# Softmax row sums moved ahead of the next group's first attention product

## The chip, the cores and the metric

One core of one Trainium2 chip. The metric is the device time of one execution in microseconds.

## The reference

Eight images of 512 channels and 32 x 32 pixels pass through a group norm, a 1 x 1 convolution, two bottleneck blocks, and a last 1 x 1 convolution with a residual. Each block is a 3 x 3 convolution, an attention over 1024 pixels with four heads of 64 channels, and a 1 x 1 convolution. What the change touches is the attention, cut to its core:

```python
qkv = conv2d(x, qkv_w, 0).reshape(b, 3, HEADS, HD, hw)
q, k, v = (qkv[:, 0], qkv[:, 1], qkv[:, 2])
logits = jnp.einsum('bhdi,bhdj->bhij', q, k + r) * HD ** (-0.5)
a = jax.nn.softmax(logits, axis=-1)
out = jnp.einsum('bhij,bhdj->bhdi', a, v)
```

## The kernel before

An attention is done in four groups (two pairs of heads, two halves of the query pixels). A group has eight key tiles, taken in pairs, so four steps. Each step computes the logits of one pair on TensorE (`l_ps`, L479), their exponentials on ScalarE (`pt`, L483), the running sum of the exponentials on VectorE (`acc`, L489 and L491), and, one step behind, the product with v on TensorE (`av_ps`, L505), which accumulates over the group's four steps.

```python
ps_big = ...tile_pool(name="ps_big", bufs=3, space=PSUM)   # logits, sums, group norm ...
ps_av  = ...tile_pool(name="ps_av", bufs=1, space=PSUM)    # the product with v

def times_v(pair):
    ...
    if j0 == 0:
        avs[g] = ps_av.tile([P, 2, HALF], F32, tag="av", name="av_ps")
    ... # 8 matmuls (16 passes) into avs[g]                        L505
    if j0 + PAIR == NJ:                  # last step of the group: the drain
        av = avs.pop(g)
        dst = ao[:, c, ts(half, HALF)]
        nc.scalar.copy(dst, av[:, 0])                              # L512
        nc.vector.tensor_tensor(dst, av[:, 1], dst, ALU.add)       # L513

def sums(g):                             # ones @ acc, to memory for the rescale
    ps = ps_big.tile([P, NQ4], F32, tag="big", name="s_ps")
    acc = accs.pop(g)
    for at_q in range(4):
        nc.tensor.matmul(ps[at_q*32:(at_q+1)*32, :], ones[:, 0:32], ...)   # L523
    nc.scalar.copy(row, ps)                                        # L529
    nc.sync.dma_start(s_dram, row[0:P:32, :])
    return s_dram

def scale(g, rs):
    nc.vector.tensor_tensor(dst, dst, rs, ALU.mult)                # L579

for i in range(len(pairs) + 1):
    if i < len(pairs):
        added = logits(pairs[i])
        g, at_q = divmod(i, NQ)
        with tc.issue_after(added.ins):
            ...
            if at_q == 0 and g > 1:
                scale(g - 2, rss.pop(g - 2))
    if i > 0:
        times_v(pairs[i - 1])
        g, j0 = pairs[i - 1][0]
        if j0 == 0:
            if g > 0:
                s_drams[g - 1] = sums(g - 1)
            with tc.issue_after(added.ins):
                behind.get(g, lambda: None)()    # other work, group norm among it
```

(`...` stands for lines left out.) PSUM is the memory into which TensorE writes. A group's product leaves its only PSUM buffer in two halves, one copied by ScalarE (L512) and one added by VectorE (L513): this is called the drain. The rescale (L579) multiplies an older group's output by the reciprocals of its row sums. A boundary is the place where one group ends and the next begins; TensorE is "held" at a boundary when the next product has to wait for the drain. The group-norm products (`gm_ps`, `gv_ps`) are small matmuls for a later group norm.

## Time and profile before

| | before |
|---|---|
| median time | 2486.34 us (2485.52 to 2486.74, 3 runs) |
| span in the profile | 2485.1 us |
| TensorE, VectorE, ScalarE busy | 97%, 60%, 38% |
| boundaries between groups, each with one set of sums (L523) | 48 |

The page's list of costly groups gives for each: busy time, mean duration of one instruction in ns, then the idle time of the engine just before it, and what ended that idle time.

```profile
L479 PE MATMUL l_ps<-q,kr 64*64 64x512 f32 x4096 | 488.0, 594 | 8.5 <-ACT pt L483 8.5
L505 PE MATMUL av_ps<-pt,vT 64*64 64x512 f32 x4096 | 486.4, 592 | 9.0 <-DVE ao L513 7.5
```

The two products of attention cost the same. Before the second one TensorE stands idle for 9.0 us in all, 7.5 of them for VectorE's half of the drain.

In the view of line L523, the sums, ScalarE waits 71.5 us in all at 47 boundaries to copy them out. ScalarE has time to spare, so this costs nothing by itself; it shows that the sums stand late in TensorE's stream.

### The profile page before, as it was taken

To read this page: it belongs to the slowest core of one execution; us is meant where nothing else is said; L and a number is where in the kernel's file an instruction comes from. 1 tells how busy PE (TensorE), PEld (TensorE's weight loads), DVE (VectorE), ACT (ScalarE), POOL (GpSimd) and SP (SyncE) were. 2 spreads that over 40 slices of the span, in tenths; PEclk is the share of its full clock that TensorE was granted. 3 is DMA by queue.
4 is the path that set the end of the run, shared out by engine and by line. 5 is a ranking of instruction groups with operands and counts; after the bars stand their busy time and mean duration, and the time that the engine had idled before them with its cause. 6 is when DMAs were issued, how large, how long until landed. Compare 5 with 4: busy or idle time off the path is not lost.

```text
span 2485.1 us, 35553 instructions
## 1 busy us (share of the span) xinstructions
PE 2416.4 (97%) x14626; PEld 1198.2 (48%) x14626; DVE 1488.6 (60%) x2482; ACT 939.7 (38%) x1280; POOL 104.9 (4%) x355
## 2 busy tenths in 40 slices
PE   6799999999999999999999999999999999999998
PEld 4436446363463634636355363644536354363533
DVE  7678554766456664666546665566564665636654
ACT  2353522525134251443414334153431525325252
POOL 1000000000100001000010000100001000010001
PEclk9899999999999999999999999999999999999999
DMA  7124014040140402304032030502205021050102
GB/s 235 61 90 157 27 39 170 14 153 10 60 149 15 152 15 85 119 14 153 14 133 76 29 134 15 181 28 77 91 10 203 10 87 43 22 191 14 69 10 65
DMA packets 82203, 200.01 MB, mean 80 GB/s; under 512 B 27889, under 2 KB 37809, under 8 KB 69745
## 3 DMA queue, kind: packets, MB, share of 16 engines
q1 hardware_dynamic: 68080, 152.00, 17.8%
q0 software_dynamic: 11808, 45.62, 5.2%
q8 instruction: 117, 1.92, 0.3%
q14 instruction: 54, 0.43, 0.1%
q10 hardware_dynamic: 2144, 0.03, 0.0%
HBM read 167.74 MB, written 29.88 MB: 80 GB/s over the span
## 4 chain that ended last, share of the span: by engine, by line
PE 86%; DVE 5%; ACT 3%; issue 2%; DMA 0%; POOL 0%; SPq 0%; ACTq 0%; DVEq 0%
PE ps L266 33%; PE av_ps L505 15%; PE l_ps L479 14%; PE c_ps L695 13%; PE v_ps L445 4%; PE m_ps L716 4%; ACT pt L483 3%; PE s_ps L523 1%; DVE ao L513 1%; PE s_ps L541 1%; ACT t L252 1%; DVE acc L491 0%; DVE acc L489 0%; DVE v_in L325 0%; DVE st L368 0%
## 5 line engine op out<-in xcount | busy, mean ns | idle before, releaser
L483 ACT ACTIVATE pt<-l_ps 128x1024 f32<-128x1024 f32 x512 | 495.1, 1023 | 230.7 <-PE l_ps L479 230.7
L491 DVE TENSOR_TENSOR acc<-acc,pt 128x1024 f32<-128x1024 f32 x384 | 469.6, 1223 | 131.8 <-ACT pt L483 108.1
L479 PE MATMUL l_ps<-q,kr 64*64 64x512 f32 x4096 | 488.0, 594 | 8.5 <-ACT pt L483 8.5
L505 PE MATMUL av_ps<-pt,vT 64*64 64x512 f32 x4096 | 486.4, 592 | 9.0 <-DVE ao L513 7.5
L695 PEld LDWEIGHTS c_ps<-v_in,u 128*128 128x128 f32 x2688 | 302.6, 192 | 11.5 <-issue 6.7
L695 PE MATMUL c_ps<-v_in,u 128*128 128x128 f32 x2688 | 303.2, 275 | 4.2 <-DVE v_in L325 4.2
L505 PEld LDWEIGHTS av_ps<-pt,vT 64*64 64x64 f32 x4096 | 153.3, 133 | 306.1 <-issue 222.1
L479 PEld LDWEIGHTS l_ps<-q,kr 64*64 64x64 f32 x4096 | 150.2, 133 | 283.1 <-issue 259.1
L266 PE MATMUL ps<-x,w 128*128 128x512 f32 x512 | 227.8, 601 | 2.2 <-DVE x L401 2.2
L266 PE MATMUL ps<-z,qkv_sb 128*128 128x512 f32 x512 | 229.3, 595 | 0.4
L266 PE MATMUL ps<-ypad,w 128*128 128x512 f32 x512 | 227.8, 594 | 0.6 <-ACT t L252 0.6
L489 DVE TENSOR_TENSOR acc<-pt 128x1024 f32<-128x1024 f32 x64 | 78.4, 1225 | 136.8 <-ACT pt L483 136.8
L266 PEld LDWEIGHTS ps<-x,w 128*128 128x128 f32 x512 | 97.1, 192 | 130.8 <-issue 127.3
L266 PEld LDWEIGHTS ps<-ypad,w 128*128 128x128 f32 x512 | 96.5, 190 | 126.0 <-issue 124.6
L433 DVE TENSOR_TENSOR kr<-ps,rw_sb 128x512 f32<-128x512 f32 x64 | 41.2, 686 | 186.0 <-PE ps L266 186.0
L252 ACT ACTIVATE t<-ps,bh,sh 128x512 f32<-128x512 f32 x58 | 42.7, 775 | 274.6 <-PE ps L266 166.8
L266 PEld LDWEIGHTS ps<-z,qkv_sb 128*128 128x128 f32 x512 | 94.7, 190 | 107.2 <-issue 91.8
L778 DVE TENSOR_TENSOR t<-t,x_res 128x512 f32<-128x512 f32 x64 | 43.8, 690 | 170.2 <-ACT t L252 142.8
L266 PE MATMUL ps<-y,w 128*128 128x512 f32 x256 | 118.0, 599 | 4.1 <-ACT t L252 4.1
L332 ACT COPY m<-c_ps 128x256 f32<-128x256 f32 x96 | 35.5, 369 | 221.2 <-PE c_ps L695 214.7
L266 PE MATMUL ps<-ylast,w 128*128 128x512 f32 x256 | 117.2, 595 | 0.0
L445 PE MATMUL v_ps<-qkv_sb,z 128*128 128x256 f32 x512 | 115.7, 379 | 0.0
(121 smaller groups left out, 1980.9 us busy)
## 6 DMA issues: line engine op xcount, KB each, us to landing
u<-u SPq DMA_DIRECT2D x84, 1024.0 KB
w<-in_cv_w_dram SPq DMA_DIRECT2D x25, 1024.0 KB
x<-in_x_dram SPq DMA_DIRECT2D x32, 512.0 KB
x_res<-in_x_dram POOLq DMA_DIRECT2D x64, 256.0 KB, 3.8
out_dram<-t POOLq DMA_DIRECT2D x62, 256.0 KB, 2.9
u<-u_new POOLq DMA_DIRECT2D x12, 1024.0 KB, 5.4
rs<-r_dram SPq DMA_DIRECT2D x96, 128.0 KB
raw<-in_m_cv_w_dram SPq DMA_DIRECT2D x8, 576.0 KB
```

The lines of the kernel that those rows point to most:

```text
L252: return nc.scalar.activation(dst, src, AF.Silu, scale=sh[:, k : k + 1], bias=bh[:, k : k + 1])
L266: nc.tensor.matmul(ps[:, half, :], w_of(k), rhs_of(k, half), start=(k == begin), stop=(k == end))
L433: nc.vector.tensor_tensor(dst, img(ps[:, half, :]), rw, ALU.add)
L445: nc.tensor.matmul(ps[:, at, :], z[:, k, ts(j0 + at, P)], qkv_sb[:, n, k, 2 * C : 3 * C], start=(k == 0), stop=(k == NM - 1),)
L479: nc.tensor.matmul(ps[kh * HD : (kh + 1) * HD, hd, :], kr[r, c, o : o + HD], q[r, c, ts(half, HALF)], start=True, stop=True,)
L483: exp = nc.scalar.activation(pt[:, i], ps, AF.Exp, scale=SCALE)
L489: return nc.vector.tensor_tensor(accs[g], pt[:, 0], pt[:, 1], ALU.add)
L491: ins = nc.vector.tensor_tensor(accs[g], accs[g], pt[:, i], ALU.add)
L505: nc.tensor.matmul(avs[g][hd * HD : (hd + 1) * HD, kh, :], vT[r, j, o : o + HD], pt[r, i, hd, :], start=(j == 0), stop=(j == NJ - 1),)
L695: nc.tensor.matmul(ps[:, row, col, :], us[i][:, k, row, col, :], vs[i][:, k, row, col, :], start=(k == 0), stop=(k == NM - 1),)
L716: nc.tensor.matmul(pss[oc][:, half, :], m2_sb[:, n, k, ts(oc, P)], ao[:, k, ts(half, HALF)], start=(k == 0), stop=(k == NM - 1),)
L778: nc.vector.tensor_tensor(t, t, res.pop(0), ALU.add)
```

## The change

The intent: at a group boundary TensorE waits for the previous group's product to be drained before the next group's first product may overwrite its only PSUM buffer. The sums are independent work that stands right behind that product. They are put ahead of it, so that they run during the wait.

```diff
                 if i > 0:
+                    g, j0 = pairs[i - 1][0]
+                    if j0 == 0 and g > 0:
+                        s_drams[g - 1] = sums(g - 1)
                     times_v(pairs[i - 1])
-                    g, j0 = pairs[i - 1][0]
                     if j0 == 0:
-                        if g > 0:
-                            s_drams[g - 1] = sums(g - 1)
                         with tc.issue_after(added.ins):
                             behind.get(g, lambda: None)()
```

## The prediction

> **What bounds the kernel now.** I read the page first for the busy shares, then the chain of work that ended last, then the waits of the lines that the change moves, and last the timeline at a boundary between two groups, because only start times show whether TensorE loses anything there.
>
> ```profile
> PE 2416.4 (97%) x14626; PEld 1198.2 (48%) x14626; DVE 1488.6 (60%) x2482; ACT 939.7 (38%) x1280; POOL 104.9 (4%) x355
> ...
> PEclk9899999999999999999999999999999999999999
> ...
> PE 86%; DVE 5%; ACT 3%; issue 2%; DMA 0%; POOL 0%; SPq 0%; ACTq 0%; DVEq 0%
> PE ps L266 33%; PE av_ps L505 15%; PE l_ps L479 14%; PE c_ps L695 13%; PE v_ps L445 4%; PE m_ps L716 4%; ACT pt L483 3%; PE s_ps L523 1%; DVE ao L513 1%; PE s_ps L541 1%; ACT t L252 1%; DVE acc L491 0%; DVE acc L489 0%; DVE v_in L325 0%; DVE st L368 0%
> ```
>
> TensorE is busy 97% of the span at full granted clock, and 86% of the chain lies on it. So a change is worth what it takes out of TensorE's own stream of starts. The one foreign entry near the sums (L523) is L513, the VectorE half of draining the attention product (av_ps), with 1% of the chain.
>
> ```profile
> L513 DVE TENSOR_TENSOR ao<-av_ps,ao x64: 680/683/693, 130.4 to 2435.1; 128x512 f32<-128x512 f32 x64
> ...
>   PEld av_ps L505: 45.2, 48
>   PE av_ps L505: 7.5, 31
> ```
>
> These are the waits on L513: weight loads of the next product waited 45.2 us at 48 boundaries, matmuls 7.5 us at 31. The two disagree, and neither is the gain. The weight-load figure counts idle time that always lies between loads (0.28 us in the steady stream); the matmul figure leaves out the time by which the modelled matmul end (1.90 us for 16) overhangs the step to the next start (1.72 us). The timeline settles it. This is one boundary, all engines but weight loads; columns are start and duration in us:
>
> ```profile
> 458.52 1.90 PE L479 MATMUL l_ps<-q,kr 64*64 64x512 f32 x16
> 458.77 0.59 ACT L512 COPY ao<-av_ps 128x512 f32<-128x512 f32 x1 [0.64 <-PE av_ps L505]
> 459.31 0.68 DVE L579 TENSOR_TENSOR ao<-ao,rs 128x512 f32<-128x512 f32 x1
> 459.62 1.94 ACT L483 ACTIVATE pt<-l_ps 128x1024 f32<-128x1024 f32 x2 [0.27 <-PE l_ps L479]
> 459.91 0.69 DVE L513 TENSOR_TENSOR ao<-av_ps,ao 128x512 f32<-128x512 f32 x1
> 460.65 1.95 PE L505 MATMUL av_ps<-pt,vT 64*64 64x512 f32 x16 [0.23 <-DVE ao L513]
> 460.68 2.55 DVE L491 TENSOR_TENSOR acc<-acc,pt 128x1024 f32<-128x1024 f32 x2
> 462.52 0.64 PE L523 MATMUL s_ps<-acc,ones 128*32 128x256 f32 x8
> 463.09 0.39 PE L374 MATMUL gm_ps<-mv,gmat 128*128 128x4 f32 x2
> ```
>
> The logits start at 458.52 and the next group's first product at 460.65: 2.13 us, against 1.72 us for an undisturbed step. TensorE is held 0.41 us. The product has one PSUM buffer (two 512-column halves), and it comes free only when VectorE ends L513 at 460.60. VectorE is late because the rescale L579 of an older group is ahead of L513 in its queue. Then the sums run, with their inputs long ready. The work that could have filled the hole stands right behind it.
>
> **What the Trainium skill says.** "Perfetto Trace Analysis", section "Tensor Engine Instruction (MATMUL, LD_WEIGHTS)", says that the reported end of a matmul is estimated, not observed, so I count start to start. The 1.90 us blocks above that begin every 1.72 us agree. "TensorE: Matmul & The Clock Gate", "Step-by-step: what each phase is for", says matmuls stay in program order and only weight loads are pulled ahead; so the sums behind a blocked product cannot slip past it. The trace agrees: none of the 48 sums starts before its product. "TensorEngine Tiling (Array Packing)", "Key Properties", says that changing the tiling mode drains TensorE. The trace shows a price: in the case without a wait, a 64*64 block followed by the 128*32 sums takes 1.83 us to the next start, not 1.72 (+0.11), and the logits after the sums take 1.77 (+0.05). "Perfetto Trace Analysis", "Optimization Strategy", ties a repeating bubble on the saturated engine to too few buffers; the single buffer of av_ps is that here.
>
> **The change, part by part.** Nothing is added or removed. At 48 boundaries (8 images, 2 blocks, 3 boundaries) the four sums (8 passes) move from behind the next group's first 16-pass product to ahead of it. The built instruction order confirms it: on TensorE the swap alone, on VectorE nothing, on ScalarE one swap of a sums copy with a weight transform in the first image, on the DMA queue only names of scratch buffers.
>
> Will the sums themselves wait? They need the last accumulate of the old group, which precedes in VectorE's queue the first accumulate of the new one (L489, which began at 458.16, before the logits), and a buffer of the three-deep PSUM ring that an exponential freed at 458.14. In the new place they have two written-out waits, one for each; both are over by 458.2, two microseconds before the sums' turn.
>
> Cost of one boundary, from the start of the logits to the start of the following product, read from the starts of all 48:
>
> Before, held: 2.13 (logits, wait) + 1.88 (product; 0.05 more than 1.83, as its first weights could not be loaded early) + 0.57 (sums) + 1.77 (next logits) = 6.35 us. After: 1.83 (logits, switch into the sums) + 0.57 (sums) + 1.77 (product) + 1.72 (logits) = 5.89 us. The drain ends at about 2.13 after the start of the logits and the product would start at 2.40, so the whole wait is covered with 0.27 us to spare. Gain 0.46 us.
>
> Before, not held (first boundary of each attention: no older group to rescale, so L513 ends at 1.70): 1.72 + 1.83 + 0.57 + 1.77 = 5.89 us. After: the same. Gain 0.
>
> Held, with a group-norm product behind it (gm_ps or gv_ps, 128*128, at the second and third boundary of the first block of seven images, 14 in all): before, the sums shield it and it adds 0.31 us. After, it stands between a 64*64 product and 64*64 logits and must pay its own switch, so 0.11 + 0.05 us are given back (estimate from the switches above). Gain 0.30 us.
>
> The count: 16 not held (0). Of the other 32, one in the first image starts at 1.84 and has a group-norm product: 0. One starts at 2.50 because the rescale waited 0.28 us for its transfer: about 0.57. Twelve regular ones with a group-norm product: 12 x 0.30 = 3.6. Eighteen regular ones without: 18 x 0.46 = 8.3. Sum 12.5 us, or 0.5% of 2486.34.
>
> Beside this, the sums' result leaves some 2 us earlier: ScalarE's copy L529, which now idles 71.5 us in all for the sums, can follow the exponentials at once. The row sums go through memory sooner. None of it is on the path: the reciprocal L567 waited for its transfer 0.9 us in all, and ScalarE is busy 38%.
>
> **The rivals.** (1) The hole moves and is not filled: the sums wait in the new place, for VectorE or for the ring. Against it stand the times above (ready two microseconds early) and VectorE's slack at the boundary (1.62 us idle before L489). It would make the gain near 0: 2486. (2) The chain's 1% on L513 is all gain, some 25 us: 2461. Against: L513's 0.69 us mostly run while the logits still do; only 0.41 us shows in the starts. (3) The matmul wait of 7.5 us is the whole gain: 2479. Against: it misses the overhang between modelled end and next start and counts 0.23 where the starts show 0.41. (4) Switching is not symmetric: the step from the sums into the product cannot load weights early, or group norm costs more than I took. For it: the trace has no case of sums followed by a product. At 0.2 us more per boundary it would eat 9.6 of the 12.5 us: 2483. (5) The saved time becomes a wait elsewhere: row-sum transfers or the next image's weights take fixed time while TensorE arrives earlier. For it: the last rescale (L579) already waits for transfers, 57.8 us over 17 times. Against: the m_ps products that need it show no matmul idle, since the filler products lie between. Worth 1 or 2 us.
>
> **Range and chances.** Prediction 2474 us. The range 2469 to 2481 holds the sum with a give-back of half (rival 4 or 5) on one side, and a gain in the not-held boundaries or smoother exponentials on the other. A 2% gain needs 50 us, four times the sum and twice the chain's share for L513; a 2% loss would need a full microsecond more at every boundary, more than the sums take. Chances: faster by over 2% 0.01, within 2% 0.98, slower 0.01.
>
> **What would show it.** Right: logits to sums 1.83 us at nearly all 48 boundaries, sums to product 0.57, product to logits 1.77, no matmul wait of L505 on L513 but for one or two; L513 gone from the chain or far smaller; the group-norm product about 0.11 us later behind its product; ScalarE's wait for L523 far below 71.5 us. Wrong: a wait of L523 for VectorE or ScalarE (rival 1); sums to product clearly above 0.57 without a wait on L513 (rival 4); the boundaries shorter as reckoned but the span not, with new waits in the 3x3 or final products (rival 5).

## The result, and the profile after

| | before | changed |
|---|---|---|
| median time | 2486.54 us (2485.52 to 2487.82, 4 runs) | 2474.05 us (2473.74 to 2474.80, 4 runs) |
| span in the profile | 2485.1 us | 2472.6 us |

The ratio of the times is 0.995 (95% interval 0.9933 to 0.9967). Ratios here and below are the mean time of one kernel's fast runs over that of the other's of the same rounds, so not quite the ratio of the medians quoted. The medians differ by 12.5 us.

The page after the change: busy shares, the chain by engine and by line, and the same two groups (granted clock 0.993, as before 0.994).

```profile
PE 2411.5 (98%) x14626; PEld 1201.4 (49%) x14626; DVE 1488.8 (60%) x2482; ACT 934.0 (38%) x1280; POOL 104.6 (4%) x355
...
PE 93%; DVE 3%; ACT 1%; issue 0%; ACTq 0%; DVEq 0%
PE ps L266 34%; PE av_ps L505 18%; PE l_ps L479 18%; PE c_ps L695 13%; PE v_ps L445 4%; PE m_ps L716 4%; PE s_ps L523 1%; PE s_ps L541 1%; ACT t L252 1%; DVE v_in L325 0%; DVE acc L491 0%; ACT pt L483 0%; DVE st L368 0%; DVE v_in L323 0%; DVE ypad L724 0%
...
L479 PE MATMUL l_ps<-q,kr 64*64 64x512 f32 x4096 | 486.1, 592 | 8.5 <-ACT pt L483 8.5
L505 PE MATMUL av_ps<-pt,vT 64*64 64x512 f32 x4096 | 487.5, 594 | 1.5 <-ACT pt L483 1.4
```

TensorE's busy time moved by only 4.9 us and its share rose: a busy share does not show the gain. What shows it is that L505 no longer waits for L513 at all (1.5 us idle remain, for an exponential), and that L513 is gone from the chain, whose TensorE share rose from 86% to 93%.

The view of L513 after, its operations and those who wait for it:

```profile
L513 DVE TENSOR_TENSOR ao<-av_ps,ao x64: 682/684/692, 130.6 to 2422.8; 128x512 f32<-128x512 f32 x64
...
  PEld av_ps L505: 12.8, 31
```

No matmul waits for the drain any more. The 12.8 us of weight loads are 31 times 0.41 us, the ordinary distance between the sums and the product's first loads, not a loss. In the view of L523 ScalarE's copy is no longer among those who wait: the 71.5 us went to nothing.

The timeline of the boundary that the prediction shows, now with the sums ahead (weight loads and queue entries left out):

```profile
457.71 1.90 PE L479 MATMUL l_ps<-q,kr 64*64 64x512 f32 x16
...
457.96 0.58 ACT L512 COPY ao<-av_ps 128x512 f32<-128x512 f32 x1 [0.64 <-PE av_ps L505]
...
458.50 0.68 DVE L579 TENSOR_TENSOR ao<-ao,rs 128x512 f32<-128x512 f32 x1
...
459.10 0.68 DVE L513 TENSOR_TENSOR ao<-av_ps,ao 128x512 f32<-128x512 f32 x1
...
459.54 0.64 PE L523 MATMUL s_ps<-acc,ones 128*32 128x256 f32 x8
...
460.11 1.95 PE L505 MATMUL av_ps<-pt,vT 64*64 64x512 f32 x16
...
461.99 0.39 PE L374 MATMUL gm_ps<-mv,gmat 128*128 128x4 f32 x2
```

Logits to sums: 459.54 - 457.71 = 1.83 us. Sums to product: 0.57 us. Product to group norm: 1.88 us. L513 ends at 459.78, a third of a microsecond before the product starts, and the product is not held. Over all 48 boundaries the starts read:

| from start to start, us | before, not held (16) | before, held (typical of 31) | changed (48) |
|---|---|---|---|
| logits to what follows | 1.72 (product) | 2.13 (product) | 1.83 (sums) |
| product to sums / sums to product | 1.83 | 1.88 | 0.57 |
| sums to logits / product to logits | 0.57 | 0.57 | 1.77 |
| next logits to product | 1.77 | 1.77 | 1.72 |
| sum | 5.89 | 6.35 | 5.89 |

(Group norm left out. The last row adds the rounded steps; unrounded, the totals are 5.88, 6.34 and 5.88 us. One boundary of the first image, at 1.84 us, stands between the first two columns, and one of the 31 was held to 2.50 us.) The sum can be checked without the start and end of the program: from the logits of boundary 4 to those of boundary 48 TensorE takes 2418.75 - 279.24 = 2139.51 us before and 2407.09 - 279.38 = 2127.71 us after, 11.80 us less. The prediction's terms for these boundaries, without the first image (0.30) and without boundary 48 itself (0.46), come to 12.5 - 0.76 = 11.7 us.

### The profile page after: what moved, and what is told of

The parts are those of the page before. It is cut to its first block, busy times and chain, and to the rows that moved or that the text cites. A ratio compares the mean times of both kernels' runs of the same rounds, so it can differ in the third digit from the quotient of the medians.

```text
span 2472.6 us, 35601 instructions
## 1 busy us (share of the span) xinstructions
PE 2411.5 (98%) x14626; PEld 1201.4 (49%) x14626; DVE 1488.8 (60%) x2482; ACT 934.0 (38%) x1280; POOL 104.6 (4%) x355
## 3 DMA queue, kind: packets, MB, share of 16 engines
q8 instruction: 117, 1.92, 0.3%
## 4 chain that ended last, share of the span: by engine, by line
PE 93%; DVE 3%; ACT 1%; issue 0%; ACTq 0%; DVEq 0%
PE ps L266 34%; PE av_ps L505 18%; PE l_ps L479 18%; PE c_ps L695 13%; PE v_ps L445 4%; PE m_ps L716 4%; PE s_ps L523 1%; PE s_ps L541 1%; ACT t L252 1%; DVE v_in L325 0%; DVE acc L491 0%; ACT pt L483 0%; DVE st L368 0%; DVE v_in L323 0%; DVE ypad L724 0%
## 5 line engine op out<-in xcount | busy, mean ns | idle before, releaser
L505 PE MATMUL av_ps<-pt,vT 64*64 64x512 f32 x4096 | 487.5, 594 | 1.5 <-ACT pt L483 1.4
L505 PEld LDWEIGHTS av_ps<-pt,vT 64*64 64x64 f32 x4096 | 152.5, 133 | 280.4 <-issue 229.5
```

The costliest lines, as they stand in the source:

```text
L505: nc.tensor.matmul(avs[g][hd * HD : (hd + 1) * HD, kh, :], vT[r, j, o : o + HD], pt[r, i, hd, :], start=(j == 0), stop=(j == NJ - 1),)
```

## The experiments

The theory: TensorE was held at 32 of 48 boundaries because VectorE's drain L513 ended too late, and the drain was late because the rescale L579 stood ahead of it. The sums do not shorten the drain; they cover it. The product starts at the later of two times, the end of the drain and the end of the sums (2.40 us behind the start of the logits). Rivals: the gain comes from sending the sums out sooner; the gain comes from fewer or cheaper changes of TensorE's tiling; the wait only moved.

All results were correct. Times are medians; the kernel before was timed in the same rounds each time (medians 2486.54 to 2487.01 us). The rounds of e1, e2, e3 and e5, of e4 and e6 to e8, and of e10 to e13 ran on three different chips by the record. The changed kernel was timed again only in the last of them (e12); a loss "on the changed kernel" is otherwise counted from its first 2474.05 us.

### The other cure: the rescale behind the drain (e1, and again e13)

The sums stay where they were. The rescale is put behind the drain in VectorE's queue.

```diff
-                    nc.vector.tensor_tensor(dst, av[:, 1], dst, ALU.add)
+                    return nc.vector.tensor_tensor(dst, av[:, 1], dst, ALU.add)
...
-                        if at_q == 0 and g > 1:
-                            scale(g - 2, rss.pop(g - 2))
                 if i > 0:
-                    times_v(pairs[i - 1])
+                    drain = times_v(pairs[i - 1])
+                    g_new, at_q = divmod(i, NQ)
+                    if i < len(pairs) and at_q == 0 and g_new > 1:
+                        with tc.issue_after(drain.ins):
+                            scale(g_new - 2, rss.pop(g_new - 2))
```

> The old order of the sums, but the rescale of the older group stands behind the drain in VectorE's queue instead of ahead of it. Theory (the product is held only because the rescale delays the drain): all 48 steps from the logits to the product become 1.72 us, the 32 held ones too; gain 30 x 0.46 + 0.2 + 0.8 = 14.8 us, so about 2471.5 us, even 2 us below the moved sums because the group norm keeps its shield. Rival A (the gain comes from sending the sums to ScalarE and memory earlier): the sums are as late as before, so no gain, 2486 us. Rival B (the hold is the drain itself, not its place in the queue): no gain either.

Measured: 2472.36 us (2471.70 to 2473.52), ratio 0.9943 (0.9929 to 0.9956). The timeline of the same boundary:

```profile
456.70 1.90 PE L479 MATMUL l_ps<-q,kr 64*64 64x512 f32 x16
...
456.95 0.59 ACT L512 COPY ao<-av_ps 128x512 f32<-128x512 f32 x1 [0.64 <-PE av_ps L505]
...
457.57 0.69 DVE L513 TENSOR_TENSOR ao<-av_ps,ao 128x512 f32<-128x512 f32 x1
...
458.17 0.68 DVE L579 TENSOR_TENSOR ao<-ao,rs 128x512 f32<-128x512 f32 x1
...
458.42 1.90 PE L505 MATMUL av_ps<-pt,vT 64*64 64x512 f32 x16
...
460.24 0.64 PE L523 MATMUL s_ps<-acc,ones 128*32 128x256 f32 x8
```

L513 now comes first and L579 second. Logits to product is 1.72 us here and at all 48 boundaries. The cause of the hold is shown: it is the rescale's place ahead of the drain. Rival A falls, as the sums are as late as in the kernel before and ScalarE still waits 56.5 us for them; rival B falls too.

### Both cures together (e2)

The changed kernel with the same shift of the rescale.

> The moved sums and the rescale behind the drain together. Theory: both cure the same hold, so nothing is added: 2474 us, within 1 us of the changed kernel. If they were separate gains they would add up to about 2460 us.

Measured: 2474.01 us (2473.08 to 2475.02), ratio 0.9949 (0.9935 to 0.9962). The two do not add up: once the sums cover the drain, an earlier drain is worth nothing. Its 48 boundaries have the same steps from start to start as the changed kernel's.

### What the group norm lost (e3, and e12 beside e13)

In the changed kernel the group-norm product stands alone between two 64*64 blocks. In e3 it is issued right behind the sums.

```diff
-                    times_v(pairs[i - 1])
                     if j0 == 0:
                         with tc.issue_after(added.ins):
                             behind.get(g, lambda: None)()
+                    times_v(pairs[i - 1])
```

> The moved sums, with the group-norm product issued straight behind the sums and ahead of the attention product. Theory (the group norm lost its shield, 0.11 + 0.05 us each at 14 boundaries): the 14 switches vanish, gain 2.2 us on the changed kernel, 2471.8 us; sums to group norm 0.57, group norm to product 0.31, product to logits 1.77 us. Rival (the 0.11 us is group norm's own wait for VectorE or for its PSUM buffer): the wait moves with it and the time stays 2474 us or grows.

Measured: 2473.10 us (2471.54 to 2473.58), ratio 0.9942 (0.9929 to 0.9956). TensorE at the same boundary:

```profile
458.29 1.90 PE L479 MATMUL l_ps<-q,kr 64*64 64x512 f32 x16
460.12 0.64 PE L523 MATMUL s_ps<-acc,ones 128*32 128x256 f32 x8
460.69 0.39 PE L374 MATMUL gm_ps<-mv,gmat 128*128 128x4 f32 x2
461.00 1.95 PE L505 MATMUL av_ps<-pt,vT 64*64 64x512 f32 x16
462.77 1.47 PE L479 MATMUL l_ps<-q,kr 64*64 64x512 f32 x12
```

Sums to group norm 0.57, group norm to product 0.31, product to logits 1.77 us: as expected, and 0.16 us less than in the changed kernel, which takes 1.88 + 0.31 us from its product to the logits and 1.77 us for them. From boundary 4 to 48 this makes 2405.72 - 279.96 = 2125.76 us against 2127.71, 1.95 us less (12 x 0.16 = 1.92). The median moved by only 1.0 us of the 2.2 expected. The rest lies outside the boundaries: this profile reaches boundary 4 0.58 us later, and such starts scatter: the two profiles of one and the same kernel, e1 and e13, reach it at 278.37 and 280.13 us. The switch cost is shown at the boundaries; in the median it is at the edge of what can be seen.

e12 is the changed kernel and e13 is e1 once more, in the same rounds.

> The changed kernel itself once more, to have it beside the next one in the same rounds: 2474 us.

> The old order with the rescale behind the drain once more, in the same rounds: 2472.4 us as in its first run, 1.5 to 2.2 us under the changed kernel, because the group norm pays no switch of its own. If the first run's lead was chance, the two are equal.

Measured: 2474.59 us (2472.97 to 2474.99) for the changed kernel and 2472.22 us (2471.98 to 2473.01) for the other cure. The lead of 1.7 us (e1 against e2) came back as 2.4 us, and from boundary 4 to 48 it is 2127.73 - 2125.80 = 1.93 us. So the version with the rescale behind the drain and the sums left in place is faster than the changed kernel by a thousandth. It cannot be told from e3: that takes 2125.76 us from boundary 4 to 48, and the ranges of the two times overlap.

### How late may the drain be? (e4, e5, e6)

An operation that changes nothing (maximum of the output with itself) is put ahead of VectorE's half of the drain: 512 columns wide in the kernel before (e4) and the changed kernel (e5), 256 wide in the changed kernel (e6).

```diff
                     nc.scalar.copy(dst, av[:, 0])
+                    d0 = dst[:, 0:512]           # e6: 0:256
+                    nc.vector.tensor_tensor(d0, d0, d0, ALU.max)
                     nc.vector.tensor_tensor(dst, av[:, 1], dst, ALU.add)
```

> The kernel before, with the same idle VectorE operation of 128x512 ahead of every drain. Theory: with the sums behind the product nothing covers the drain, so the 32 held boundaries lose all of it (0.62 us each, 20 us) and the 16 others nearly all (0.65 us each with the late weight load, 10 us): about 2516 us, three times the loss of the moved sums. Rival (a slower drain costs both kernels the same): the same 11 us as there, 2497 us.

> The moved sums, with an idle VectorE operation of 128x512 (maximum of the output with itself, result unchanged) put ahead of every drain, some 0.62 us. Theory (the product starts at the later of 2.40 us behind the logits and the end of the drain, now about 2.13 + 0.62 = 2.75): the 32 boundaries with a rescale are held by about 0.35 us, the 16 without (drain at 2.32) by nothing; loss about 11 us, 2485 us. Rival (the sums do not cover the drain but only shift it): all of it shows, 48 x 0.62 = 30 us, 2504 us. Rival (drain is far off the path after the change): 2474 us.

> The moved sums, with an idle VectorE operation of only 128x256 ahead of every drain, some 0.35 us. Theory: the drain then ends about 2.48 us behind the logits where the product could start at 2.40, so 32 boundaries are held by under 0.1 us, loss 0 to 3 us, 2474 to 2477 us: the 0.27 us to spare takes up most of it. Without that slack the loss would be 32 x 0.35 = 11 us, 2485 us.

Measured: e4 2527.90 us (+40.9 on the kernel before), e5 2495.85 us (+21.8 on the changed kernel), e6 2486.48 us (+12.4). All three losses are larger than expected. The VectorE timeline of e5 shows why (the added lines shift the numbers: L581 is the rescale, L514 the extra operation, L515 the drain; the sums are L525 below):

```profile
459.75 0.68 DVE L581 TENSOR_TENSOR ao<-ao,rs 128x512 f32<-128x512 f32 x1
460.35 0.68 DVE L514 TENSOR_TENSOR ao<-ao 128x512 f32<-128x512 f32 x1
461.14 0.69 DVE L515 TENSOR_TENSOR ao<-av_ps,ao 128x512 f32<-128x512 f32 x1
```

I had put the extra operation at 0.62 us, from independent operations that start 0.60 us apart. But the drain reads what the extra operation wrote, so it starts 0.79 us behind it, 0.11 us after its end (a wait instruction of its own, 21 ns, lies between). The product also starts 0.15 us after the end of the drain in these three runs, not 0.05 as in the kernel before. The traces show what differs: in these runs, and in e10 and e11 below, the view of L505 lists `PEldq EVENT_SEMAPHORE` x48, each 51 ns (PEldq is the sequencer of the weight loads), a wait that stands as an instruction of its own ahead of the product's first weight load; the kernel before and the changed one have none there. In e4 it begins 0.04 us after the end of the drain, lasts 0.05 us, and the product starts 0.06 us after it. So the edits added about 0.09 us beside the operation itself. The size was wrong; the rule held. TensorE in e5 and in e4:

```profile
458.95 1.93 PE L479 MATMUL l_ps<-q,kr 64*64 64x512 f32 x16
460.80 0.64 PE L525 MATMUL s_ps<-acc,ones 128*32 128x256 f32 x8
461.98 1.95 PE L505 MATMUL av_ps<-pt,vT 64*64 64x512 f32 x16 [0.54 <-DVE ao L515]
```

```profile
464.49 1.90 PE L479 MATMUL l_ps<-q,kr 64*64 64x512 f32 x16
467.51 1.95 PE L505 MATMUL av_ps<-pt,vT 64*64 64x512 f32 x16 [1.12 <-DVE ao L515]
```

The product starts 461.98 - 458.95 = 3.03 us behind the logits in e5 and 467.51 - 464.49 = 3.02 us in e4: with a drain late enough, the order of the sums makes no difference to the product, and in e5 the sums inside that time cost nothing. At the boundaries without a rescale both start it at 2.50 us.

The sums follow. In e5 a boundary with a rescale loses 0.60 us (0.63 in the product's start, 0.03 regained in the product itself, 1.74 us for 1.77), one without loses 0.07: 32 x 0.60 + 16 x 0.07 = 20.3 us, and three boundaries that were held longer than the others add 1.9 us; measured 21.8. In e4 it is 0.88 us with a rescale and 0.78 + 0.05 without: 32 x 0.88 + 16 x 0.83 = 41.4 us; measured 40.9. In e6 VectorE's drain ends 2.60 us behind the logits and the product starts at 2.75: 0.62 us later than in the kernel before (2.13), but only 0.35 us later than in the changed one (2.40). The difference is the 0.27 us that the prediction had to spare. By its time alone e6 looks like the expectation's case without slack (2485 us); only the starts tell the two apart.

### A drain that is late by about the slack (e10, e11)

VectorE's half of the drain in four independent pieces of 128 columns.

```diff
-                    nc.vector.tensor_tensor(dst, av[:, 1], dst, ALU.add)
+                    for q in range(4):
+                        nc.vector.tensor_tensor(
+                            dst[:, ts(q, 128)], av[:, 1, ts(q, 128)], dst[:, ts(q, 128)], ALU.add
+                        )
```

> The moved sums, with VectorE's half of the drain cut into four operations of 128x128 that do not depend on each other. From the starts of the 128x512 (0.60 us apart) and 128x256 operations (0.34 apart) four pieces should end about 0.23 us later than one. Theory (0.27 us to spare under the sums): the drain ends at about 2.36 us behind the logits, still under the 2.40 where the product can start, so nothing is lost: 2474 us. If there were no slack: 32 x 0.23 = 7 us, 2481 us.

> The kernel before with the same drain in four pieces. Theory: nothing covers it, so each of 48 boundaries starts its product some 0.2 us later: 9 to 11 us, about 2497 us, where the moved sums lose nothing.

Measured: e11 2499.92 us, 13.1 us more than the kernel before; its products start at 2.41 us where they were held and at 1.90 where not (32 x 0.28 + 16 x (0.18 + 0.05) = 12.6 us). That is more than the 9 to 11 us expected: the drain itself ends 0.2 us later (2.26 us behind the logits where it was 2.07), as expected, but the separate wait instruction adds 0.09 us. So the drain is late by about the whole slack and not by less. e10: 2476.15 us (2474.07 to 2476.30), by its median 1.6 us more than the changed kernel in the same rounds (e12, 2474.59 us). In its profile (the run of 2474.07 us) sums to product is 0.57 to 0.59 us at all boundaries but one of the third image. There the rescale waited 0.59 us for its transfer, the drain behind it ended late, and the product started 0.15 us after that end, as after every late drain of these runs; the profile puts the 0.62 us of TensorE's wait down to an exponential, but its time fits the drain. So the slack is shown at the boundaries, where the kernel before loses 0.28 us and the changed one 0.02. Why the other runs of e10 tend to be 2 us longer, I cannot say from one profile.

### Sums in the neighbours' tiling (e7, e8)

If switching costs 0.16 us each time, sums that need no switch should be cheaper. The sums of every group are computed as those of the last group are: in 64*64 tiles, the two halves of the partitions apart, added afterwards from memory.

```diff
-                ps = ps_big.tile([P, NQ4], F32, tag="big", name="s_ps")
-                for at_q in range(4): ...                   # 128*32 tiles, 256 columns
+                ps = ps_big.tile([P, 2, HALF], F32, tag="big", name="s_ps")
+                for kh in range(2):
+                    for hd in range(2):
+                        nc.tensor.matmul(ps[hd*HD:(hd+1)*HD, kh, :], ones[r], acc[r, hd, :], ...)
+                # two copies and two transfers; last_total(g, s_dram) adds the halves
```

> The moved sums computed in the tiling of their neighbours (64*64, 64x512, four products as for the last group; two halves added afterwards from memory by a small VectorE operation), so that TensorE need not switch. Theory (0.11 into the sums and 0.05 out of them are the switch, and 0.57 holds another part of it): logits to sums 1.72, sums 0.43, product 1.72 us; 0.30 us less at each of 48 boundaries, 14 us, 2460 us; the drain at 2.13 is just covered at 2.15. Rival (the sums cost their own work, not a switch): as many columns in twice as wide products are no less work, 2474 us or more, and ScalarE's two copies of 0.59 us in place of one of 0.37 hold the exponentials.

> The same 64*64 sums in the old place behind the product. Theory: the switch is saved here as well (14 us), but the 32 holds of 0.41 us stay: about 2472 us, 12 us above the same sums in the new place. If the switch were what the change saved, this one would equal the 64*64 sums in the new place.

Measured: e7 2482.21 us (8.2 us more than the changed kernel), e8 2501.36 us (14.4 us more than the kernel before). TensorE in e7 at a plain boundary:

```profile
597.60 1.90 PE L479 MATMUL l_ps<-q,kr 64*64 64x512 f32 x16
599.32 1.04 PE L523 MATMUL s_ps<-acc,ones 64*64 64x512 f32 x8
600.18 1.90 PE L505 MATMUL av_ps<-pt,vT 64*64 64x512 f32 x16
```

The switch is indeed gone: logits to sums is 1.72 us, product to logits 1.72. But the sums take 0.86 us, not the 0.43 I wrote. My expectation was wrong by its own data: 16 passes of this shape take 1.72 us, so eight take 0.86. Against 0.11 + 0.57 + 0.05 = 0.73 us in the old tiling this is 0.13 us more at each of 48 boundaries, 6 us. Besides, in e7 two products and in e8 eight start later than their kind, by up to 3.4 us in e8 (boundary 2, 5.49 us behind its logits, where the rescale waits 2.8 us for its transfer). e8 is 19 us slower than e7 where I expected 12: its holds stay, and with sums that are both longer and late, rescales come late too: at seven of the eight, and at both of e7's, the rescale waited for its transfer (0.03 to 2.83 us). So the rival that the change saved switches falls. The first rival of e7 (the sums cost their work) is right about the size: the switch is real but smaller than what avoiding it costs.

## Why the prediction was right

The predicted time was 2474 us and the measured one 2474.05. That agreement is better than the working deserves, since starts of the first image alone scatter by a microsecond. In the two profiles two misses cancel: up to boundary 4 the changed kernel loses 0.14 us where 0.30 were to be gained, and from boundary 48 to the end it gains 0.79 us where 0.46 were expected. That part is luck. Point by point:

- **The bound, and start-to-start reading.** Right. The chain is still TensorE's, now 93%, and the gain is the difference of starts. Neither the 7.5 us of the matmul wait nor the 1% of the chain (25 us) was the gain: 12.5 us was.
- **Readiness of the sums.** Right: logits to sums is 1.82 or 1.83 us at all 48 boundaries in the changed kernel, with no wait for VectorE or the PSUM ring. Rival 1 falls. (In e12, the same kernel again, one boundary of the first image took 2.24 us; the logits block itself was stretched there.)
- **Cost of a boundary, 5.89 us.** Right to 0.01 us, both for the held and the not-held kind. The assumption that switching costs the same in the new order, which rival 4 doubted, held: 0.57 and 1.77 us. e5, e6, e10 confirm the 0.27 us to spare. Two readings beside it were loose: at the held boundaries the drain ends 2.07 us behind the logits (the prediction's own lines give 460.60 - 458.52 = 2.08), and 2.13 is where the product starts; and at the others it ends at 1.56 us, not 1.70. The sums rest on starts and are not touched. The boundary held to 2.50 us gained 0.67 us, not the 0.57 that was put down for it.
- **The cause of the late drain.** In the prediction it was read off one boundary; e1 shows it by removing it.
- **Group norm gives back 0.16 us at 14 boundaries.** Right: 1.88 us to the group norm instead of the sums' shield, and e3 and e13 recover 1.9 us over twelve of them.
- **Nothing comes back elsewhere (rival 5).** Right for boundaries 4 to 48 (11.80 us of 11.7). In the first image the changed profile is at boundary 4 0.14 us later where the sum had 0.30 us gained; the starts of other runs there scatter by more.
- **The row sums leave sooner, off the path.** Right in the changed kernel; e7 and e8, where rescales waited for their transfers, show that the time of these transfers is close to mattering.

What the experiments corrected is not in the prediction's sums but in my expectations of the experiments: the cost of a dependent VectorE operation (e4 to e6) and of 64*64 sums (e7, e8).

## What to carry to other kernels

When the busiest engine waits at a repeated place, first read the wait from start to start, then look for work already in its queue behind the wait whose inputs are ready, and also for work on the releasing engine that could stand behind the release: here each cures the same 0.41 us, and together they give no more than one. Such a cover is worth the smaller of the hole and the moved work (0.46 us here, where the hole was smaller; 0.74 us at a boundary with a rescale in e5 against e4, where the sums with their switches, 0.73 us, were smaller), and what stood protected by the moved work (here the group norm, behind a change of tiling) then has to pay for its own change of tiling.

## What the Trainium skill lacked or had wrong

- "TensorEngine Tiling (Array Packing)", "Key Properties", says that changing the tiling mode drains TensorE but gives no price. Here going from 64*64 to 128*32 or 128*128 costs 0.11 us and coming back 0.05 us at the next block (1.83 and 1.77 us in place of 1.72). e7 removes both.
- Beyond the general advice to let blocking dependencies start sooner, no page that I read has it that a repeating bubble at a single PSUM buffer can be cured by order alone: here twice, without another buffer, by 12.5 us (order on TensorE) and by 14.3 us (order on VectorE, e1).
- "VectorE: DVE Perf Modes", "The DRAIN you can't avoid", gives a length for the flush after each operation and a case in which semaphores cost nothing extra, but no figure for a successor that reads the result: 128x512 operations of 0.68 us that do not depend on each other start 0.60 us apart here, and one that reads the other's result starts 0.79 us behind it, 0.11 us after its end, with a wait instruction between them (e5). Without such an instruction the reader starts 0.03 us after the end (L369 behind L368 in the kernel before).
